# Rounding and clipping y through an int8 tile on ScalarE, with a new plan, in a cross-attention and BitNet-FFN kernel

## The chip, the cores and the metric

The kernel runs on one core of one Trainium2 chip. The core has five engines that matter here, each with its own instruction queue, executed in order: TensorE (PE; matmuls into PSUM), VectorE (DVE), ScalarE (ACT), GpSimd (POOL), and SyncE (SP), which here only issues DMA transfers. The metric is device time in microseconds (us). A "batch" below is one of 32 slices of 128x512 that pass through the whole network one after the other.

## What is computed

The input x has 32 batches of 128 channels x 512 positions; ctx has the same shape. Per batch:

```python
x = x + xattn(layernorm(x), ctx)      # 8 heads of 16 channels, 512 x 512 scores a head
x = x + ffn(layernorm(x))             # 128 rows, 512 -> 2048 -> 512

def act_quant(x):                     # 8 bits, one scale a row
    scale = 128 / clip(max|x|, 1e-5)
    return clip(round(x * scale), -128, 127) / scale

def ffn(x):
    gate, up = act_quant(x) @ wq(w_gate).T, act_quant(x) @ wq(w_up).T
    y = fwht(silu(gate) * up)         # Walsh-Hadamard transform over 2048
    return act_quant(y) @ wq(w_down).T
```

wq makes the weights ternary (-1, 0, 1) with one scale. The change concerns act_quant(y), the second rounding and clipping, and the multiplication by w_down.

## The kernel before

**Staging.** The work on each batch is cut into tasks, written as Python generators (`s_load`, `s_a`, `s_mpe`, `s_eact`, ... `s_dn`). Before each instruction or small block, a generator yields what it needs: a buffer of a ring (`"get"`), an event (`"on"`), or an engine and the duration that the planner should charge (`"pe", 0.234`; `"dma", 0.73`). The class `Plan` runs all generators together and keeps for each engine the time at which it would come free. At each step it takes the instruction that could start earliest; among those that could start within `eps` (`epspe` on PE) it takes the one of lowest rank. The rank is a number of the task from the table `CFG` (separate ones for the first four batches, `.h`, and the last four, `.z`) plus `T` times the batch; on PE the mode in which the array was last used is preferred by `stick`. This order is fixed when the program is built and becomes the order of every engine's queue. So `CFG` and the charged durations set the order of everything, and on the chip an engine can't overtake its own queue.

**Modes of PE.** Scores use two 48-row or 50-row strips of the array at once ("half"), the projections and the product with the values use quarter-column strips ("cols"), all else the whole array ("full").

**One batch on PE, by the names of the profile.** Projections of q and k (L556, L557) and v (L636) into `pf`. Scores are computed twice: `pS` (L726; 128 queries by 512 keys for two heads, of which DVE takes the maximum at L741; in the first three batches every other one goes through `pf` and L746 instead) and, transposed and with the maximum subtracted, `pT` (L796), which ACT turns into P by exp (L809). 16 of each a batch. `pav` (L830) is the product of P and v, eight blocks a batch. Then the output projection (L948), gate and up (L1013, WGQ and WUQ, four blocks each), the transposes of z (L1117), the Hadamard products (L1156, L1157), small transposes for the row maximum and its reciprocal (L1195, L1215, "yb"), and the down product (L1274, two blocks of eight). pS and pT have one buffer each, `pf` three, which nearly everything else shares.

**Around the change.** `s_yv` copies the transformed y (128 x 2048 floats, one buffer, ring `y`) from PSUM (L1171). `s_am` takes its row maximum on DVE (L1184). `s_q` multiplies y by the scale (L1232, POOL or DVE, in place, two halves of 1024). `s_q1` (L1242, ACT) adds 12582912, which rounds a float to an integer. `s_q2` (L1256, ACT) forms max(0, (12582912 + 127) - y), that is 127 minus the rounded and clipped value, and writes it as bf16 into `yq` (two buffers); only then is `y` free. `s_dn` multiplies yq by the ternary weights `WDQ`, and since every element is 127 minus what is wanted, one more matmul a batch (L1275) subtracts 127 times the column sums of the weights: `NEG` (2 rows of constants) times `CS` (the sums, split into two bf16 numbers). The result has the wrong sign, which a factor of -1 in the row scale (L1223) undoes. The column sums come once, after the weights are made ternary, from 16 matmuls (L502), four operations of DVE and one transfer (L506 to L515).

**The weights.** 12 tiles of 1 MB are loaded (`s_w`), their absolute values summed (L451), scaled and rounded (L475 on ACT or L477), clipped (L485) and converted to fp8 (L493). The first gate matmul waits for the last of them. Tiles use the rings z0, z1 and y, which the FFN needs later.

Of the kernel before, what the change touches and what calls it, by code (L numbers as in the profile page):

```python
# [10 lines left out]
F32 = mybir.dt.float32  # L11
FR = mybir.dt.float32r
BF = mybir.dt.bfloat16
F8 = mybir.dt.float8e4
AF = mybir.ActivationFunctionType
# [10 lines left out]
    "a": 17204.8,  # L26
    "a.h": 56888.9,
    "a.z": 14936.6,
    "a2": 4110.6,
    "a2.h": 10733.7,  # L30
    "a2.z": 4091.9,
    "a3": -1064.4,
    "a3.h": 4876.9,
    "a3.z": 2422.1,
    "am": 4773.1,
    "am.h": 13803.0,
    "am.z": -44218.1,
    "bf": 3144.9,
    "bf.h": 24712.8,
    "bf.z": 19590.3,  # L40
    "const": 14934.4,
    "const.h": 15491.8,
    "const.z": 4076.0,
    "dn": 4293.7,
    "dn.h": 4871.1,
    "dn.z": 21179.4,
    "eact": -36632.4,
    "eact.h": -37814.4,
    "eact.z": -1863.9,
    "eav": 11135.5,  # L50
    "eav.h": 4223.8,
    "eav.z": 32251.8,
    "epe": -40145.6,
    "epe.h": -40187.6,
    "epe.z": -39869.7,
    "gact": 23899.5,
    "gact.h": -26090.9,
    "gact.z": -36563.3,
    "gpe": 56880.8,
    "gpe.h": 18311.9,  # L60
    "gpe.z": 6005.8,
    "hi": -25784.5,
    "hi.h": -26246.1,
    "hi.z": 4960.2,
    "hm": -21491.6,
    "hm.h": -24541.6,
    "hm.z": -28755.2,
    "init": -37791.2,
    "init.h": -23577.8,
    "init.z": -24582.5,  # L70
    "lo": 1897.6,
    "lo.h": 4758.2,
    "lo.z": -37078.3,
    "load": 23789.4,
    "load.h": 4770.3,
    "load.z": -31350.6,
    "mdve": 1736.2,
    "mdve.h": 4251.6,
    "mdve.z": -25448.7,
    "mfin": -25604.8,  # L80
    "mfin.h": 4075.5,
    "mfin.z": 6355.4,
    "mpe": -26070.7,
    "mpe.h": -37503.9,
    "mpe.z": -21599.3,
    "o": -25785.8,
    "o.h": 35362.7,
    "o.z": -786.3,
    "o2": -37005.1,
    "o2.h": -41684.7,  # L90
    "o2.z": -24211.2,
    "q": 13848.2,
    "q.h": -39189.8,
    "q.z": 4318.1,
    "q1": 11956.7,
    "q1.h": 4753.0,
    "q1.z": 21160.0,
    "q2": 1023.0,
    "q2.h": -21667.4,
    "q2.z": -23754.1,  # L100
    "st": -47909.0,
    "st.h": -35889.1,
    "st.z": 21989.2,
    "u": 26418.5,
    "u.h": 5310.5,
    "u.z": 24337.0,
    "udve": 18718.4,
    "udve.h": 12493.6,
    "udve.z": -34405.8,
    "upe": 29615.8,  # L110
    "upe.h": 19928.1,
    "upe.z": 14589.9,
    "v": 27752.8,
    "v.h": 57650.1,
    "v.z": 53459.6,
    "w": 35469.7,
    "w.h": -19469.2,
    "w.z": 18308.4,
    "w1": 24353.6,
    "w1.h": 18083.3,  # L120
    "w1.z": -34718.8,
    "w2": 28388.6,
    "w2.h": 5547.9,
    "w2.z": 12473.5,
    "w3": 31248.0,
    "w3.h": 19526.9,
    "w3.z": 3962.9,
    "w4": 25647.7,
    "w4.h": 6555.5,
    "w4.z": 20517.4,  # L130
    "yv": -26156.9,
    "yv.h": 11959.1,
    "yv.z": 33180.6,
    "zt": 13824.7,
    "zt.h": 15480.3,
    "zt.z": -26679.3,
    "T": 5.6,
    "eps": 0.019,
    "pen": 9.6,
    "stick": 4685.6,  # L140
    "epspe": 0.21,
# [161 lines left out]
def xattn_ffn(  # L303
# [41 lines left out]
    MAG7 = const.tile([128, 1], F32, name="MAG7")  # L345
    nc.vector.memset(MAG7, MAGIC + 127.0)
# [10 lines left out]
    CW = const.tile([128, 388], F32, name="CW")  # L357
    WQ, WK, WVT, BRP, MASK = CW[:, 0:128], CW[:, 128:256], CW[:, 256:384], CW[:, 384:386], CW[:, 386:387]
    NEGC = CW[:, 387:388]
# [15 lines left out]

    ob = const.tile([128, 1], BF, name="ob")
    nc.vector.memset(ob, 1.0)
    NEG = const.tile([2, 128], BF, name="NEG")
    CS = const.tile([2, 512], BF, name="CS")
# [30 lines left out]
    def s_init():  # L410
        yield "on", "cw"
        yield "dve", 0.2
        nc.vector.tensor_scalar(NEG, ones[0:2, :], NEGC[0:2], None, ALU.mult)
# [17 lines left out]
    def s_w():  # L431
        for n in range(12):
            m, k = divmod(n, 4)
            src = srcs[m][0][k]
            yield "get", WR[n % 4]
            yield "dma", 2.9
            w = fp.tile([128, 2048], F32, name=WR[n % 4], bufs=2 if WR[n % 4] == "z0" else 1)
            nc.sync.dma_start(out=w.rearrange("p (j i) -> p j i", j=4) if m == 2 else w, in_=src)
            WT[n] = w
            p.marks["w", n] = p.done  # L440
            p.now = p.done - 2.9
# [46 lines left out]
    def s_w4():  # L488
        for n in range(12):
            m, k = divmod(n, 4)  # L490
            yield "on", "w3", n
            yield "act", 1.95
            nc.scalar.activation(srcs[m][1][:, k, :], WT.pop(n), AF.Identity, bias=NMAG, saturate=False)  # L493
            p.put(WR[n % 4])
            if k == 3:
                p.mark("wr", m)
        yield "get", "y"
        yield "get", "pf"
        yield "pe", 3.5
# [3 lines left out]
        yield "dve", 0.6  # L503
        w = fp.tile([128, 2048], F32, name="y")
        ca, cb = w[0:1, 0:512], w[0:1, 512:1024].bitcast(BF).rearrange("p (a f) -> p a f", a=2)
        nc.vector.tensor_scalar(ca, pc[0:1, :], 1.0 / 64.0, MAGIC, ALU.mult, ALU.add)  # L506
        yield "dve", 0.6, "port"
        nc.vector.tensor_scalar(cb[:, 0], ca, -MAGIC, None, ALU.add)
        yield "dve", 0.6, "port"
        nc.vector.tensor_scalar(ca, ca, -MAGIC, -64.0, ALU.add, ALU.mult)  # L510
        yield "dve", 0.6
        nc.vector.tensor_tensor(cb[:, 1], pc[0:1, :], ca, ALU.add)
        p.put("pf")
        yield "dma", 0.1
        nc.sync.dma_start(out=CS, in_=cb)  # L515
        p.now = p.done
        p.put("y")
        p.mark("cs")
# [19 lines left out]
    def s_load():  # L538
        for b in range(NB):
            s = st[b]  # L540
            yield "at", b
            yield "get", "xt"
            yield "get", "ct"
            yield "get", "cv"
            yield "dma", 0.73
            s["x"] = xp.tile([128, T], F32, name="xt")
            nc.sync.dma_start(out=s["x"], in_=x[b])
            yield "dma", 0.73
# [25 lines left out]
    def s_a2():  # L574
        for b in range(NB):
# [43 lines left out]
            yield "dma", 1.6, 0.45  # L619
            nc.sync.dma_start(out=xo[:, 1:4:2], in_=xf[:, 1:4:2])  # L620
            yield "dma", 1.6, 0.45
# [26 lines left out]
    def s_a3():  # L648
        for b in range(NB):
# [21 lines left out]
            yield "dma", 1.6, 0.45  # L671
            nc.sync.dma_start(out=xo[:, 0:4:2], in_=xf[:, 0:4:2])
            yield "dma", 1.6, 0.45
# [169 lines left out]
    def s_u():  # L843
        for u in range(NU):
# [26 lines left out]
            yield "dma", 0.73, 0.45, 0.7  # L871
# [14 lines left out]
    def s_o():  # L886
        for b in range(NB):
# [3 lines left out]
            if b in SHORT:  # L891
                yield "dma", 0.73, 0.45, 1.2
# [18 lines left out]
            yield "dma", 0.1, 0.45, 0.6  # L911
# [4 lines left out]
            yield "dma", 0.73, 0.45, 1.2  # L916
# [3 lines left out]
            yield "dma", 0.73, 0.45, 1.2  # L920
# [7 lines left out]
            yield "dma", 0.1, 0.45, -1.0  # L928
# [4 lines left out]
            yield "dma", 0.73, 0.45, 0.5  # L933
# [241 lines left out]
    def s_am():  # L1175
        for b in range(NB):
# [46 lines left out]
            nc.vector.tensor_scalar(yc, yc, SW[:, 2:3], -1.0, ALU.mult, ALU.mult)  # L1223
# [11 lines left out]
    def s_q1():  # L1235
        for b in range(NB):
            yield "at", b
            for hf in range(2):
                yield "on", "q", b, hf
                yield "act", 1.05  # L1240
                y = st[b]["y"][:, 8 * hf : 8 * hf + 8]
                nc.scalar.activation(y, y, AF.Identity, bias=MAG)  # L1242
                p.mark("q1", b, hf)

    def s_q2():
        for b in range(NB):
# [3 lines left out]
            for hf in range(2):  # L1250
# [5 lines left out]
                nc.scalar.activation(s["yq"][:, w], s["y"][:, w], AF.Relu, bias=MAG7, scale=-1.0)  # L1256
                p.mark("yq", b, hf)
            p.put("y")

    def s_dn():  # L1260
        for b in range(NB):
# [3 lines left out]
            if b == 0:  # L1265
                yield "on", "cs"
# [8 lines left out]
            nc.tensor.matmul(ps, NEG, CS, start=False, stop=True)  # L1275
# [7 lines left out]
            yield "dma", 0.73  # L1283
# [20 lines left out]
def _layout(i):  # L1304
# [12 lines left out]
    mask = np.zeros((128, 2), f)  # L1317
    mask[[48, 49, 112, 113], 0] = -1.0
    mask[0:2, 1] = -127.0 * 64.0, -127.0
# [34 lines left out]
```

## Time and profile before

| | |
|---|---|
| median of 3 runs | 1439.01 us (1437.6 to 1448.16) |
| the profiled execution | 1444.41 us, of it 1442.5 us between its first and last instruction (the span) |
| mean granted clock of TensorE | 0.95 |
| busy share of PE, DVE, ACT, POOL | 94%, 82%, 82%, 69% |
| transfers | 214 MB, 148 GB/s |
| L1275, the correction | 32 matmuls, 384 ns each |
| L502, the column sums | 16 matmuls, from 188.1 us on |
| L1242 and L1256, rounding and clipping | 64 each, 1138 ns each |
| last pS and last pT | 1313 us and 1359 us |

How to read it: times are from the first instruction on. Each row of a group gives the line, the engine, the operation, the tile written and the tiles read, and the shapes; then the total busy time, the mean of one, and how long the engine was idle just before. Matmuls are pipelined: the next starts before the former has ended, so the distance from start to start tells what one costs, not its duration. PEclk is the clock that the throttle granted to PE, in tenths. The chain of waits follows the execution back from its last instruction, at each step to what released it.

### The profile page before, as it was taken

What the parts mean: (1) busy time and instruction counts of PE and PEld (TensorE: products, weight loads), DVE (VectorE), ACT (ScalarE), POOL (GpSimd) and SP (SyncE); (2) the same over time, 40 slices, a digit from 0 to 9 for tenths busy, and PEclk for the clock granted to TensorE, in tenths of its full rate; (3) what the DMA queues carried; (4) which work ended last, traced back from release to release, by engine and by line L of the source; (5) the groups of instructions that cost most, each with busy time, mean ns of one, the idle gap of its engine ahead of it and who ended that gap; (6) DMA issues with size and microseconds to landing.
All of it is one profiled execution on the core that took longest, in us unless ns stands there. A gap on an engine that the chain in (4) does not pass through costs nothing.

```text
span 1442.5 us, 21845 instructions
## 1 busy us (share of the span) xinstructions
PE 1353.4 (94%) x7454; PEld 529.8 (37%) x7454; DVE 1179.0 (82%) x1759; ACT 1189.0 (82%) x1574; POOL 994.7 (69%) x781
## 2 busy tenths in 40 slices
PE   3788899999999999999999999999999999999875
PEld 2222233433334333333333344333333343433332
DVE  2875878888898889888888888888888888886784
ACT  5688978888888888888888888888888888889643
POOL 3122229977777777887777787887777788769550
PEclk7596899999999999999999999999999999999986
DMA  8967555555445555555545555555554554321000
GB/s 285 282 201 245 158 159 160 151 152 143 134 147 163 171 171 174 161 153 148 136 134 154 171 167 175 168 162 156 137 141 140 161 166 153 95 65 49 21 15 15
DMA packets 136315, 214.15 MB, mean 148 GB/s; under 512 B 36746, under 2 KB 38924, under 8 KB 135180
## 3 DMA queue, kind: packets, MB, share of 16 engines
q1 hardware_dynamic: 136204, 212.75, 49.7%
q8 instruction: 59, 0.97, 0.3%
q14 instruction: 52, 0.43, 0.1%
HBM read 106.94 MB, written 93.31 MB: 139 GB/s over the span
## 4 chain that ended last, share of the span: by engine, by line
PE 84%; DVE 7%; ACT 4%; DMA 2%; issue 2%; POOL 0%; SPq 0%; ACTq 0%; DVEq 0%; POOLq 0%
PE pav L830 17%; PE pf L1013 15%; PE pT L796 14%; PE pS L726 10%; PE pf L1274 8%; PE pf L1117 4%; PE pf L556 4%; PE pf L1156 3%; ACT P L809 2%; DVE M L741 2%; PE pf L1157 2%; PE pf L948 2%; PE pf L636 2%; DVE ya L1184 1%; PE pf L1275 1%
## 5 line engine op out<-in xcount | busy, mean ns | idle before, releaser
L741 DVE TENSOR_REDUCE M<-pS 128x2 f32<-128x1024 f32 x488 | 595.0, 1219 | 105.0 <-PE pS L726 103.1
L1097 POOL TENSOR_TENSOR z<-z 128x512 f32<-128x512 f32 x491 | 619.0, 1283 | 68.5 <-DVE z L1068 48.5
L809 ACT ACTIVATE P<-pT 128x1024 f32<-128x1024 f32 x512 | 523.2, 1022 | 148.2 <-PE pT L796 146.4
L830 PE MATMUL pav<-P,va 128*32 128x512 f32 x2048 | 283.6, 625 | 0.0
L796 PE MATMUL pT<-qs,ks 50*128 50x512 f32 x1024 | 259.0, 500 | 17.1 <-ACT P L809 16.5
L726 PE MATMUL pS<-ks,qs 48*128 48x512 f32 x976 | 227.2, 458 | 14.8 <-DVE M L741 9.9
L796 PEld LDWEIGHTS pT<-qs,ks 50*128 50x128 f32 x1024 | 98.1, 188 | 240.3 <-ACT P L809 149.9
L1232 POOL TENSOR_TENSOR y<-y,YB 128x1024 f32<-128x1024 f32 x60 | 140.9, 2369 | 34.9 <-ACT YB L1218 34.9
L1013 PEld LDWEIGHTS <-xqT 128*128 128x128 bf16 x1024 | 91.8, 100 | 155.7 <-issue 84.8
L726 PEld LDWEIGHTS pS<-ks,qs 48*128 48x128 f32 x976 | 95.3, 190 | 117.8 <-issue 39.6
L532 POOL TENSOR_TENSOR arstd<-arstd,MHALF 128x1 f32<-128x1 f32 x32 | 18.6, 580 | 170.4 <-DVE arstd L529 134.8
L1013 PE MATMUL pf<-WGQ,xqT 128*128 128x512 fp8e4 x512 | 133.4, 386 | 1.0 <-ACT z L1043 0.6
L1274 PE MATMUL pf<-WDQ,yq 128*128 128x512 fp8e4 x512 | 125.4, 389 | 8.6 <-ACT yq L1256 8.5
L1184 DVE TENSOR_REDUCE ya<-y 128x128 f32<-128x1024 f32 x64 | 127.1, 1986 | 6.6 <-ACT y L1171 6.3
L1013 PE MATMUL pf<-WUQ,xqT 128*128 128x512 fp8e4 x512 | 127.0, 381 | 0.1
L1068 DVE TENSOR_TENSOR z<-z,pf 128x512 f32<-128x512 f32 x128 | 84.6, 675 | 12.9 <-PE pf L1013 8.7
L1140 DVE TENSOR_TENSOR lo<-pf,hi 128x512 fp32r<-128x512 f32 x128 | 85.7, 675 | 6.0 <-ACT hi L1129 5.9
L1043 ACT ACTIVATE z<-pf,tk 128x512 f32<-128x512 f32 x128 | 83.7, 685 | 7.4 <-PE pf L1013 4.7
L1129 ACT CAST hi<-pf 128x512 fp32r<-128x512 f32 x128 | 74.6, 588 | 17.9 <-PE pf L1117 17.9
L1171 ACT COPY y<-pf 128x512 f32<-128x512 f32 x128 | 71.9, 585 | 13.6 <-PE pf L1157 13.3
L1117 PE MATMUL pf<-CM,z 128*128 128x128 f32 x512 | 82.0, 286 | 0.0
L1274 PEld LDWEIGHTS <-yq 128*128 128x128 bf16 x512 | 46.1, 99 | 89.7 <-ACT yq L1256 22.5
(129 smaller groups left out, 1791.5 us busy)
## 6 DMA issues: line engine op xcount, KB each, us to landing
xd<-X SPq DMA_DIRECT2D x128, 512.0 KB
qs<-xd SPq DMA_DIRECT2D x128, 192.0 KB
ks<-xd SPq DMA_DIRECT2D x128, 192.0 KB
ud<-U SPq DMA_DIRECT2D x62, 256.0 KB
xt<-x SPq DMA_DIRECT2D x32, 256.0 KB
ct<-cx SPq DMA_DIRECT2D x32, 256.0 KB
RR<-R SPq DMA_DIRECT2D x64, 128.0 KB
xr<-x SPq DMA_DIRECT2D x32, 256.0 KB
```

Of the source, the lines that this page charges most:

```text
L726: nc.tensor.matmul(ps[e], qs[w, t, bass.ts(qt, 128)], ks[w, t, :], start=True, stop=True)
L741: nc.vector.tensor_reduce(m, ps[2], AX.X, ALU.max)
L796: nc.tensor.matmul(ps[:, e], ks[w, t, bass.ts(kt, 128)], qs[w, t, :], start=True, stop=True)
L809: nc.scalar.activation(P, TQ[u, n], AF.Exp, scale=0.25)
L830: nc.tensor.matmul(av[32 * h : 32 * h + 32, :], va[:, kt, 4 * hf + h, :], P[:, e], start=(kt == 0), stop=(kt == 3),)
L1013: nc.tensor.matmul(ps, xqT[:, k, :], W[:, k, bass.ts(c, 512)], start=(k == 0), stop=(k == 3))
L1097: E[p.eng].tensor_tensor(ix(dv, k), ix(av, 0), ix(av, 1), o)
L1117: nc.tensor.transpose(ps[:, i, :], st[b]["z"][:, bass.ts(4 * c + i, 128)], EYE)
L1140: nc.vector.tensor_tensor(t, F.pop(("z", b, c)), F["hi", b, c].bitcast(F32), ALU.subtract)
L1184: nc.vector.tensor_reduce(ya[:, h], s["y"][:, 8 * h : 8 * h + 8].rearrange("p j t -> p t j"), AX.X, ALU.max, apply_absolute_value=True,)
L1232: E[p.eng].tensor_tensor(y, y, st[b]["YB"].to_broadcast([128, 8, 128]), ALU.mult)
L1274: nc.tensor.matmul(ps, s["yq"][:, j, :], WDQ[:, j, :], start=(j == 0), stop=False)
```

## The change

The first of the two passes of ACT now copies the scaled y into an int8 tile `yi` (new, one buffer), and the conversion does the rounding and the clipping. The second copies `yi` to bf16. yq then holds the values themselves, so `NEG`, `CS`, the column sums, the correction matmul and the factor -1 go. `y` is free after the first pass instead of the second. The durations that the planner charges for most transfers are raised (a 256 KB tile 0.73 to 0.85, a weight tile 2.9 to 3.5, the stores of xd 1.6 and 0.45 to 1.7 and 0.9), some landing times are changed, and all numbers of `CFG` are new, `T` and `eps` among them.

```diff
 CFG = {
-    "a": 17204.8,
...
-    "T": 5.6,
-    "eps": 0.019,
-    "pen": 9.6,
-    "stick": 4685.6,
-    "epspe": 0.21,
+    "a": 21145.3,
...
+    "T": 65.3,
+    "eps": 0.0,
+    "pen": 36.3,
+    "stick": 12961.1,
+    "epspe": 0.23,
 }
...
-            yield "dma", 2.9
+            yield "dma", 3.5
             w = fp.tile([128, 2048], F32, name=WR[n % 4], bufs=2 if WR[n % 4] == "z0" else 1)
...
-        yield "get", "y"
-        yield "get", "pf"
-        yield "pe", 3.5
-        pc = ps_f.tile([128, 512], F32, name="pf")
-        for j in range(NI):
-            nc.tensor.matmul(pc[0:1, :], ob, WDQ[:, j, :], start=(j == 0), stop=(j == NI - 1))
...
-        nc.sync.dma_start(out=CS, in_=cb)
-        p.now = p.done
-        p.put("y")
-        p.mark("cs")
...
-            yield "dma", 0.73
+            yield "dma", 0.85
             s["x"] = xp.tile([128, T], F32, name="xt")
...
-            yield "dma", 1.6, 0.45
+            yield "dma", 1.7, 0.9
             nc.sync.dma_start(out=xo[:, 1:4:2], in_=xf[:, 1:4:2])
...
-            nc.vector.tensor_scalar(yc, yc, SW[:, 2:3], -1.0, ALU.mult, ALU.mult)
+            nc.vector.tensor_scalar(yc, yc, SW[:, 2:3], None, ALU.mult)
...
                 yield "on", "q", b, hf
+                if hf == 0:
+                    yield "get", "yi"
                 yield "act", 1.05
-                y = st[b]["y"][:, 8 * hf : 8 * hf + 8]
-                nc.scalar.activation(y, y, AF.Identity, bias=MAG)
+                if hf == 0:
+                    st[b]["yi"] = fp.tile([128, NI, 128], I8, name="yi", bufs=RINGS["yi"])
+                w = slice(8 * hf, 8 * hf + 8)
+                nc.scalar.copy(st[b]["yi"][:, w], st[b]["y"][:, w])
                 p.mark("q1", b, hf)
+            p.put("y")
...
-                nc.scalar.activation(s["yq"][:, w], s["y"][:, w], AF.Relu, bias=MAG7, scale=-1.0)
+                nc.scalar.copy(s["yq"][:, w], s["yi"][:, w])
                 p.mark("yq", b, hf)
-            p.put("y")
+            p.put("yi")
...
-                yield "pe", 1.73 + 0.22 * g
+                yield "pe", 1.73
                 for j in range(8 * g, 8 * g + 8):
-                    nc.tensor.matmul(ps, s["yq"][:, j, :], WDQ[:, j, :], start=(j == 0), stop=False)
-            nc.tensor.matmul(ps, NEG, CS, start=False, stop=True)
+                    nc.tensor.matmul(ps, s["yq"][:, j, :], WDQ[:, j, :], start=(j == 0), stop=(j == NI - 1))
```

More of the change, by code (lines that the diff above doesn't have):

```diff
@@ L14 @@
 F8 = mybir.dt.float8e4
+I8 = mybir.dt.int8
 AF = mybir.ActivationFunctionType
@@ new lines @@
+    "a.h": -13181.5,
+    "a.z": 1173.4,
+    "a2": -17104.5,
+    "a2.h": 690.4,
+    "a2.z": 42446.1,
+    "a3": -3175.8,
+    "a3.h": -8664.4,
+    "a3.z": 16459.6,
+    "am": 161.0,
+    "am.h": 17364.9,
+    "am.z": 32182.3,
+    "bf": 18683.0,
+    "bf.h": 31269.3,
+    "bf.z": 35303.2,
+    "const": -5501.7,
+    "const.h": 37755.7,
+    "const.z": 1763.1,
+    "dn": 239.1,
+    "dn.h": -21980.0,
+    "dn.z": 42699.2,
+    "eact": -7602.6,
+    "eact.h": -40084.8,
+    "eact.z": -1227.4,
@@ new lines @@
+    "eav": -18087.6,
+    "eav.h": -36108.9,
+    "eav.z": 38280.9,
+    "epe": -45496.9,
+    "epe.h": -38542.2,
+    "epe.z": -33211.5,
+    "gact": -4441.9,
+    "gact.h": 32995.2,
+    "gact.z": -46212.5,
+    "gpe": 53791.6,
+    "gpe.h": 14740.7,
+    "gpe.z": 54572.1,
+    "hi": -15301.6,
+    "hi.h": -5849.9,
+    "hi.z": 53342.2,
+    "hm": 18328.4,
+    "hm.h": -17814.5,
+    "hm.z": -41074.9,
+    "init": -43982.4,
+    "init.h": -42277.6,
+    "init.z": -13781.6,
+    "lo": -34328.7,
@@ new lines @@
+    "lo.h": -4433.6,
+    "lo.z": -40564.4,
+    "load": -36992.5,
+    "load.h": -44212.0,
+    "load.z": 43264.4,
+    "mdve": 999.3,
+    "mdve.h": -35953.7,
+    "mdve.z": 18143.4,
+    "mfin": -13986.7,
+    "mfin.h": -6279.4,
+    "mfin.z": -13213.6,
+    "mpe": -38114.1,
+    "mpe.h": -37525.8,
+    "mpe.z": -42237.2,
+    "o": -6480.8,
+    "o.h": 16244.1,
+    "o.z": 34116.5,
+    "o2": -36848.5,
+    "o2.h": -12371.4,
+    "o2.z": -12361.7,
+    "q": 36512.0,
+    "q.h": -15314.2,
+    "q.z": -41040.2,
@@ new lines @@
+    "q1": 42319.9,
+    "q1.h": 18458.6,
+    "q1.z": -5657.8,
+    "q2": -8876.8,
+    "q2.h": 21172.4,
+    "q2.z": 16920.5,
+    "st": -39351.8,
+    "st.h": -11680.5,
+    "st.z": -37439.4,
+    "u": -6996.8,
+    "u.h": -5670.2,
+    "u.z": -7564.8,
+    "udve": -3685.7,
+    "udve.h": 16214.8,
+    "udve.z": -38407.0,
+    "upe": 8177.0,
+    "upe.h": 31488.8,
+    "upe.z": 36033.6,
+    "v": 30497.8,
+    "v.h": -4196.4,
+    "v.z": -47392.4,
+    "w": 37879.4,
+    "w.h": -40543.6,
+    "w.z": -13715.2,
@@ L142 @@
+    "w1": 18646.4,
+    "w1.h": 31573.4,
+    "w1.z": -36044.3,
+    "w2": 42721.7,
+    "w2.h": 36222.1,
+    "w2.z": -43436.0,
+    "w3": 53243.0,
+    "w3.h": 42675.6,
+    "w3.z": -42266.9,
+    "w4": -77.4,
+    "w4.h": -36686.9,
+    "w4.z": -36683.9,
+    "yv": -6876.1,
+    "yv.h": -3275.6,
+    "yv.z": 52586.2,
+    "zt": 1199.1,
+    "zt.h": -3401.9,
+    "zt.z": -47936.5,
+    "T": 65.3,
[3 more added lines that the diff above has]
+    "epspe": 0.23,
 }
@@ L344, in xattn_ffn @@
     nc.vector.memset(NMAG, -MAGIC)
-    MAG7 = const.tile([128, 1], F32, name="MAG7")
-    nc.vector.memset(MAG7, MAGIC + 127.0)
     zeros = const.tile([128, 1], F32, name="zeros")
@@ L355, in xattn_ffn @@
     kss = [sp.tile([128, 2, T], FR, name=f"ks{i}") for i in range(4)]
-    CW = const.tile([128, 388], F32, name="CW")
+    CW = const.tile([128, 387], F32, name="CW")
     WQ, WK, WVT, BRP, MASK = CW[:, 0:128], CW[:, 128:256], CW[:, 256:384], CW[:, 384:386], CW[:, 386:387]
-    NEGC = CW[:, 387:388]
     CM = const.tile([128, 642], F32, name="CM")
@@ L374, in xattn_ffn @@
     SW = const.tile([128, 3], F32, name="SW")
[L376 to L379, printed above, removed]
     p = Plan(nc, RINGS, CFG)
@@ L440, in s_w @@
             p.marks["w", n] = p.done
-            p.now = p.done - 2.9
+            p.now = p.done - 3.5
     def s_w1():
```

153 lines of the change are left out of this document (14 added, 139 removed), and 2 rows, old and new, of the table RINGS.

## The prediction

> **What bounds the kernel now.** I read the page's busy shares and slices first, then the stages, then TensorE's rows in one steady batch, then the chain of waits.
>
> ```profile
> PE 1353.4 (94%) x7454; PEld 529.8 (37%) x7454; DVE 1179.0 (82%) x1759; ACT 1189.0 (82%) x1574; POOL 994.7 (69%) x781
> ...
> PE   3788899999999999999999999999999999999875
> ...
> PEclk7596899999999999999999999999999999999986
> ```
>
> TensorE (PE) is full from the sixth slice to the last but three. The stage table (columns: stage, its length, then busy time and count by engine, clock, DMA share, GB/s) says how full:
>
> ```profile
> 0.00:250.00 250.00, 196.75 (x948) 70.28 (x949) 170.12 (x261) 194.66 (x235) 88.41 (x81) 0.80 0.68 214
> 250.00:1300.00 1050.00, 1047.85 (x6014) 413.29 (x6012) 913.60 (x1349) 907.57 (x1222) 834.88 (x649) 1.00 0.52 150
> ...
> 1358.60:1442.50 83.90, 55.63 (x221) 25.88 (x219) 55.45 (x86) 41.28 (x58) 24.40 (x16) 0.79 0.03 13
> ```
>
> So a head of 250 us at a clock of 0.80, 1,050 us in which PE idles 2 us, and a tail of 84 us after the last transposed score (at 1358.65). A busy PE isn't PE at its peak, so I price it by start-to-start distances. From the timeline of the steady part:
>
> ```profile
> 713.16 0.40 PE L726 MATMUL pS<-ks,qs 48*128 48x512 f32 x2
> 713.49 1.06 PE L830 MATMUL pav<-P,va 128*32 128x512 f32 x8
> ...
> 717.64 0.39 PE L1275 MATMUL pf<-CS,NEG 2*128 2x512 bf16 x1
> 717.96 0.50 PE L796 MATMUL pT<-qs,ks 50*128 50x512 f32 x2
> ```
>
> A score block (two matmuls, pT or pS) advances PE by 0.33 us in a run of such blocks, a pav block by 1.00, the correction matmul by 0.32 (717.64 to 717.96). The correction stands at 717.64 in one batch and at 757.80 in the next: 40.1 us a batch. Pricing every block so, with its mode switch, gives 39.7 us a batch, so only 0.4 us is waiting; over the whole kernel it gives 1279 us, the rest being about 91 us of waiting and half clock in the head, 14 in the middle, 45 from 1300 on, and 8 before the first matmul. **The bound is PE's own order**; what comes free on ScalarE (ACT) doesn't shorten it.
>
> **The change, part by part.** All sums are against the profiled execution: 1442.5 us span, 1444.4 with what lies around it, 5.4 above the median of the runs (1439.0).
>
> *Removed on PE.* 32 corrections x 0.32 = 10.2 us, all on the saturated engine. The 16 column-sum matmuls (L502) start at 188.11 and the next score at 191.66: 3.5 us, and the score it holds back is waited for by the exp. Sum **-13.7**. The four VectorE (DVE) operations and the 2 KB transfer behind the column sums, and two memsets, lie beside this; nothing.
>
> *The two ACT passes.* They stay 64 + 64 of 128x1024. L1242 and L1256 took 1138 ns each, with a bias tile. No row has a float-to-int8 or int8-to-bf16 pass. Bounds: 1053 (L451, absolute value of 1024 floats) and 2 x 585 = 1170 (two 512-wide copies from PSUM, L1171); at most 2369, what GpSimd needs for 1024 (L1232). I take 1.06. ACT then frees 128 x 0.08 = 10 us, off the path: ACT idled in the steady part for want of PE's scores (80.9 us between 400 and 1130). At 2369 it would add 158 us to ACT, 4.9 a batch on top of some 35 of 40, and ACT would become the bound; the conversion is one pass of the same engine over as many elements, so I leave that to a rival. [...]
>
> *y comes free a pass earlier.* L1232, L1242 and L1256 work on a single y. After the change the first pass releases it, 1.1 us (one pass) sooner. In the steady part PE isn't waiting for y, so nothing; in the last three or four batches about 1.1 us each, **-4**.
>
> *The order.* The priorities of every task and the planner's transfer prices change too, so every queue is reshuffled. I laid the two programs' PE lists side by side and priced each block as above.
>
> - Work per batch is the same blocks less one. But there are 223 lone score blocks instead of 158; a lone one advances PE by 0.43 (a pT at 728.93, the next block at 729.36), 0.10 more than in a run: +6.8. Quarter-column blocks straight after full-array ones go from 24 to 52 at 0.09: +2.6. Other switches +0.3. Sum **+9.7**.
> - Scores closer than their consumers allow. pT and pS have one buffer each. The chain shows the shortest turn of each:
>
> ```profile
> 87.63 0.45 PE pT L796 x2
> 88.08 0.02 issue
> 88.10 1.03 ACT P L809
> 89.13 0.04 issue
> 89.18 0.50 PE pT L796 x2
> ...
> 173.05 0.45 PE pS L726 x2
> 173.49 0.02 issue
> 173.51 1.24 DVE M L741
> 174.75 0.04 issue
> 174.80 0.51 PE pS L726 x2
> ```
>
> pT to pT 1.55 us, pS to pS 1.75. I summed PE's own work between successive ones, from the first gate matmul on. Before: 3 pT gaps and no pS gap under 1.45, 37 pS gaps of 1.45 to 1.75; shortfalls 1.6 us (pT) and 2.6 (pS). After: 21 and 12, many of 0.66 (score pairs in a row with nothing between them, around pT 127 to 135 and 401 to 407 of 512), and 146 pS gaps of 1.45 to 1.75; shortfalls 9.7 and 19.8. Behind a waiting score stands all of PE. The increase is 17 us by pS alone, 25 if the pT shortfalls never coincide with them: **+20**. The old order in the middle lost 14 where the gaps alone said 4, so it may be more; if PE's order was drawn where it idles anyway, less: 8 to 30.
>
> *Head.* Same weights, same 54 exps before the first silu; the w_down loads go to SP's queue ahead of the fifth batch's inputs and that batch's RR swap, and 4.9 us more attention precedes the first gate matmul. About 30 of the head's 91 us aren't explained by score turns, and PE's waits that name a DMA are 12 (CW 7.8, ks 4.4). CW comes first in both. Bounds -12 and +8, taken as **0**, since the ks waits are small and more weight loads ahead delay inputs.
>
> [...]
>
> *Tail.* The last pT has 10.8 us less PE work before it, but 4 instead of 3 batches still have their y scaling to come (28 instead of 29 yb transposes done, 49.8 instead of 44.5 us of PE work left). One batch at the end takes 20 us. That is a wash: 84 us becomes 84 to 95 with the last pT earlier by 10.8. With y free earlier: PE's idle here goes from 39 to about 35, the -4 above.
>
> Sum: -13.7 + 9.7 + 20 + 0 - 4 = **+12**, and 4 more for the 4.4 us by which the head's score turns grow by the same count (63.9 instead of 59.5): **+16**. Span 1458, median of the runs 1439 + 16 = **1455**.
>
> **Rivals.**
>
> 1. *The corrections' saving is kept* (ends not slower). It decides if the head reordering is worth 12 or more, because inputs are asked for when the traces say they land, and the shortfalls cost 8: -13.7 + 9.7 + 8 - 12 - 4 + 4 = -8, 1431; with the shortfall at 14, 1437. For it: 0.68 DMA share and a 0.80 clock in the head. Against: only 12 us of PE's waits there name a DMA.
> 2. *Rings add to the bunched scores.* Three pf buffers serve every block but the scores and pav; where attention runs ahead, ACT's exps delay the FFN copies that free them. Shortfalls at 30 and a tail of 95 us (+7): -13.7 + 9.7 + 30 + 4 + 7 = +37 at worst; 1470 at half of that excess. For it: the measured 14 against 4.
> 3. *The int8 passes aren't priced like others.* At 1.2 us more a pass ACT is full; 32 x 2 to 4 us gives 1500 and more. Nothing in the trace points there.
>
> **How the numbers follow.** Forecast 1455 (1442 to 1466): chance 0.55, about 0.33 of it beyond +1%. Rival 1: 0.28, of which 0.08 is below -1% and the rest within. Rival 2: 0.15. Rival 3: 0.02. One per cent is about what a measurement of this kernel can tell from no change (1424.6 to 1453.4). So faster 0.08, same 0.42, slower 0.50. The range takes in most of rivals 1 and 2: 1431 to 1472. The likeliest case sits close to the line between same and slower.
>
> **What would show it.** No L1275 and L502, their 13.7 us gone. Both passes near 1.06 us. PE idle, or long pT and pS advances, in the middle where attention bunches, with ACT named for pT and DVE for pS; a steady batch of 40.3 to 41.2 us instead of 40.1. Last pT at 1365 to 1380. The forecast is wrong if the middle runs at 39.7 a batch or less, if the first gate matmul comes well before 186, or if the tail after the last pT is under 75 us.

## The result, and the profile after

The changed kernel takes **1519.5 us** (median of 4 runs, 1515.2 to 1526.6); the kernel before took 1441.3 beside it (1437.6 to 1448.2). The ratio is 1.054, with a 95% interval of 1.048 to 1.060: 78 us slower. The forecast of 1455 had the right side and missed the size; 1519 lies far outside its range of 1431 to 1472. The profiled execution of the changed kernel took 1519.85 us, 1518.0 of it the span, 75.5 more than the span before.

In the page after, the busy shares and the slices that answer to those shown of before:

```profile
PE 1373.5 (90%) x7406; PEld 535.4 (35%) x7406; DVE 1185.5 (78%) x1753; ACT 1197.1 (79%) x1575; POOL 992.2 (65%) x779
...
PE   3788799999899999999999999999899999998475
...
PEclk7578899999999999999999999999999999999786
```

No engine has more to do in any way that matters: DVE, ACT and POOL are busy for the same time within 1%, and PE's 20 us more come with 48 matmuls fewer, so its matmuls last longer in the record (185.5 ns in the mean instead of 181.6). All shares fall because the span grew. So the 75.5 us are waiting, apart from what more switches of PE's mode may cost. The last three digits of the PE row (475) say where some of it is: a hole in the tail.

The stage table of after, cut at the first gate matmul and at the start of the last pT (columns: stage, its length, busy time and count of PE, PEld, DVE, ACT, POOL, then clock, DMA share, GB/s):

```profile
0.00:196.60 196.60, 135.60 (x641) 47.65 (x642) 125.27 (x192) 152.62 (x179) 47.87 (x46) 0.74 0.71 232
196.60:1395.80 1199.20, 1166.76 (x6504) 453.76 (x6502) 989.95 (x1461) 995.59 (x1325) 900.49 (x704) 1.00 0.46 139
1395.80:1518.00 122.20, 71.18 (x262) 34.02 (x262) 70.31 (x101) 48.89 (x71) 43.88 (x30) 0.76 0.03 11
```

The same cuts in the kernel before are at 185.7 and 1358.7 of 1442.5; its first two rows (the third stands in the prediction):

```profile
0.00:185.70 185.70, 133.60 (x604) 46.44 (x604) 121.75 (x188) 145.39 (x172) 47.91 (x46) 0.73 0.74 236
185.70:1358.60 1172.90, 1164.17 (x6633) 457.44 (x6631) 1001.80 (x1485) 1002.28 (x1345) 922.36 (x719) 1.00 0.50 144
```

So the loss splits in three:

| stage | before | after | difference |
|---|---|---|---|
| head, to the first gate matmul | 185.7 | 196.6 | +10.9 |
| middle, to the last pT | 1172.9 | 1199.2 | +26.3 |
| tail, after it | 83.9 | 122.2 | +38.3 |

In the steady stretch one batch after the other has the same length. The row of the small transpose yb (L1184), of which there is one a batch, in a window of the steady stretch, after and (L1215) before:

```profile
L1184 PE MATMUL pf<-CM,yb x5: 328/332/332, 822.8 to 989.4; 128*128 128x128 f32 x5
...
L1215 PE MATMUL pf<-CM,yb x5: 329/330/330, 820.1 to 980.7; 128*128 128x128 f32 x5
```

From the first to the fifth are four batches in 166.6 us, **41.65 a batch**; the forecast said 40.3 to 41.2, and it was 40.15 before.

The new passes are where they were expected (rows of L1215 and L1230: minimum, median and maximum in ns, first and last start):

```profile
L1215 ACT CAST yi<-y x64: 1028/1045/1071, 261.1 to 1506.1; 128x1024 int8<-128x1024 f32 x64
...
L1230 ACT CAST yq<-yi x64: 1027/1044/1068, 264.8 to 1508.0; 128x1024 bf16<-128x1024 int8 x64
```

The forecast's own value was 1.06. Which of the two sides is int8 makes no difference that these rows show.

**The tail.** What PE and the others wait for in it (waits after 1395.8: who, for whom, us in total, times, longest):

```profile
PE pf L1248 <- ACT yq L1230: 28.4, 6, 16.8
DVE lo L1109 <- ACT hi L1098: 20.8, 3, 16.6
ACT yi L1215 <- POOL y L1201: 19.9, 5, 17.4
```

Three long waits of about 17 us, on three engines, that end one in the other: the second half of a down product waits for yq, whose pass stands behind yi on ACT, and yi waits for POOL's scaling of y. In the tail of the kernel before, the longest wait for yq (of PE's weight loads; 17.0 here) is 5.3 us:

```profile
PEld L1274 <- ACT yq L1256: 8.7, 2, 5.3
```

The timeline of after (start, us, engine, line, operation) shows why:

```profile
1394.43 2.37 POOL L1201 TENSOR_TENSOR y<-y,YB 128x1024 f32<-128x1024 f32 x1
1396.76 17.74 POOL L1066 TENSOR_TENSOR z<-z 128x512 f32<-128x512 f32 x14
1414.45 2.34 POOL L1201 TENSOR_TENSOR y<-y,YB 128x1024 f32<-128x1024 f32 x1
...
1398.34 1.04 ACT L1230 CAST yq<-yi 128x1024 bf16<-128x1024 int8 x1
1416.83 1.04 ACT L1215 CAST yi<-y 128x1024 int8<-128x1024 f32 x1 [17.44 <-POOL y L1201]
```

Between the two halves of one batch's scaling stand 14 butterflies of a later batch in POOL's queue. POOL works through them first, 17.74 us in all, ACT waits 17.4 us with its next copies queued behind, and y, of which there is one buffer, stays taken. The distance from one yb transpose to the next, 27.1, 21.1 and 20.4 us at the end of the kernel before, is here 48.1, 25.4, 22.8 and 18.9, with four batches to go instead of three.

**The head.** The last tile of w_down is scaled at 176.5 and clipped at 179.4 before. After (timeline, two queues):

```profile
184.88 2.10 ACT L466 ACTIVATE y<-y,MAG,SC 128x2048 f32<-128x2048 f32 x1
...
187.71 0.75 DVE L849 SCALAR_TENSOR_TENSOR x<-pf,BO,xr 128x512 f32<-128x512 f32 x1 [0.56 <-PE pf L917]
...
191.77 1.78 DVE L476 TENSOR_SCALAR y<-y 128x2048 f32<-128x2048 f32 x1
```

The scaling starts 8 us later, in an ACT queue that is busy with exps and copies ahead of it, and the clip stands for 5 us in DVE's queue behind the residual sum (L849), its statistics and two maxima. That is this tile's place in the two queues; DVE idles less than 1 us between.

The first gate matmul doesn't wait for this tile itself on the chip, though. It reads only w_gate's weights and xqT, and the rows of PE just ahead of it are these:

```profile
195.71 0.81 PE L695 MATMUL pS<-ks,qs 48*128 48x512 f32 x2 [0.50 <-DVE M L710]
196.46 0.38 PE L732 MATMUL pf<-CM,M 128*16 128x128 f32 x1
196.63 0.63 PE L982 MATMUL pf<-WGQ,xqT 128*128 128x512 fp8e4 x1
```

It starts when the blocks ahead of it in PE's queue are through. The tile counts by way of the order: the generator of the gate waits for the event that the last w_down tile is converted, and by the planner's clock that event moved from 171.2 to 186.8, so more attention was put ahead of the gate. From the last sum over w_down's absolute values (148.8 before, 153.2 after, 151.0 and 155.4 in two other profiles of the same head) to the first gate matmul PE has 134 matmuls in 36.9 us before and 173 in 43.3 after: 4.7 us more of advance and 1.7 more of idle time. In the unshortened profiles of the new order without the correction this stretch takes 43.3 to 43.8. The other 4.4 us lie ahead of it; the largest difference there is PE's wait for the absolute sums of w_gate near 30 us, 11.7 us (L448) against 3.4, which is only 6.9 in another profile of the same head.

### The profile page after: what moved, and what is told of

It reads as the page before. It is cut to its first block, busy times and chain, and to the rows that moved or that the text cites. A ratio compares the mean times of both kernels' runs of the same rounds, so it can differ in the third digit from the quotient of the medians.

```text
span 1518.0 us, 21675 instructions
## 1 busy us (share of the span) xinstructions
PE 1373.5 (90%) x7406; PEld 535.4 (35%) x7406; DVE 1185.5 (78%) x1753; ACT 1197.1 (79%) x1575; POOL 992.2 (65%) x779
## 5 line engine op out<-in xcount | busy, mean ns | idle before, releaser
L1066 POOL TENSOR_TENSOR z<-z 128x512 f32<-128x512 f32 x489 | 616.9, 1284 | 66.4 <-DVE z L1037 41.2
L695 PE MATMUL pS<-ks,qs 48*128 48x512 f32 x976 | 235.8, 476 | 24.7 <-DVE M L710 16.5
L1153 DVE TENSOR_REDUCE ya<-y 128x128 f32<-128x1024 f32 x64 | 126.8, 1981 | 11.0 <-ACT y L1140 10.9
L908 POOL TENSOR_TENSOR N<-N,RB 128x512 f32<-128x512 f32 x31 | 39.6, 1278 | 97.7 <-DMA RB<-rd 62.6
L501 POOL TENSOR_TENSOR arstd<-arstd,MHALF 128x1 f32<-128x1 f32 x32 | 19.4, 606 | 128.1 <-DVE arstd L498 124.7
L1086 PE MATMUL pf<-CM,z 128*128 128x128 f32 x512 | 86.1, 290 | 13.2 <-DVE xq L947 5.2
L1037 DVE TENSOR_TENSOR z<-z,pf 128x512 f32<-128x512 f32 x128 | 86.1, 677 | 14.3 <-PE pf L982 13.7
L1012 ACT ACTIVATE z<-pf,tk 128x512 f32<-128x512 f32 x128 | 84.3, 683 | 10.4 <-PE pf L982 9.6
L1140 ACT COPY y<-pf 128x512 f32<-128x512 f32 x128 | 75.5, 591 | 19.6 <-PE pf L1126 18.8
```

What stands on the lines that cost most here:

```text
L695: nc.tensor.matmul(ps[e], qs[w, t, bass.ts(qt, 128)], ks[w, t, :], start=True, stop=True)
L1037: nc.vector.tensor_tensor(zc, zc, F.pop(("u", b, c)), ALU.mult)
L1066: E[p.eng].tensor_tensor(ix(dv, k), ix(av, 0), ix(av, 1), o)
L1153: nc.vector.tensor_reduce(ya[:, h], s["y"][:, 8 * h : 8 * h + 8].rearrange("p j t -> p t j"), AX.X, ALU.max, apply_absolute_value=True,)
```

## The experiments

Two kinds are used. In the first, the order of every queue is kept and only the instructions in it change: the generators yield exactly what they yielded, so the planner decides the same. In the second, the planner's input is changed and the order is drawn anew.

**The arithmetic in the old order.** The kernel before, with all its yields; the passes, the factor and the down product are those of the changed kernel, and the instructions of the column sums are dropped (their durations stay in the plan).

```diff
-                y = st[b]["y"][:, 8 * hf : 8 * hf + 8]
-                nc.scalar.activation(y, y, AF.Identity, bias=MAG)
+                nc.scalar.copy(st[b]["yi"][:, w], st[b]["y"][:, w])
...
-                nc.scalar.activation(s["yq"][:, w], s["y"][:, w], AF.Relu, bias=MAG7, scale=-1.0)
+                nc.scalar.copy(s["yq"][:, w], s["yi"][:, w])
...
-            nc.tensor.matmul(ps, NEG, CS, start=False, stop=True)
```

> The order of every queue stays that of the kernel before; only the arithmetic changes: int8 tile, copy to bf16, no correction matmul, no column sums, factor +1. Theory A (the loss lies in the new order, the arithmetic itself gains): 1441 less 10.2 (32 corrections at 0.32) less 3.5 (column sums) = 1427.5, and up to 4 less where y comes free a pass earlier in the tail, so 1423 to 1430; tail after the last pT 80 to 84 us, first gate matmul near 185. Theory B (the int8 passes or the earlier release of y cost the time): 1480 or more. Theory C (PE waits elsewhere, so that taking 13.7 us of matmuls out brings nothing): 1438 to 1444.

Measured: **1429.8 us** against 1442.4 of the kernel before beside it, ratio 0.992 (0.989 to 0.995). The stage table of its profile:

```profile
0.00:183.70 183.70, 130.81 (x605) 44.94 (x606) 121.56 (x187) 145.11 (x172) 47.79 (x46) 0.75 0.74 238
183.70:1350.00 1166.30, 1154.17 (x6589) 453.77 (x6587) 998.97 (x1481) 995.42 (x1345) 921.49 (x719) 1.00 0.51 145
1350.00:1432.80 82.80, 53.95 (x216) 25.67 (x215) 55.33 (x86) 39.62 (x58) 24.39 (x16) 0.79 0.04 13
```

All three stages are a little shorter than before, none is longer. So the new arithmetic by itself is a gain of some 12 us, the new order a loss of 90 (1519.5 - 1429.8), and theory A holds. It is also the version that beats both kernels.

**The correction alone.** The same, but with the old two passes; the output, with no correction, is too large by 127 column sums.

```diff
-            nc.tensor.matmul(pc[0:1, :], ob, WDQ[:, j, :], start=(j == 0), stop=(j == NI - 1))
...
-            nc.tensor.matmul(ps, NEG, CS, start=False, stop=True)
```

> The order of the kernel before with its own two passes of ScalarE; only the correction matmul and the column sums (with their four VectorE operations and the transfer) are left out, so the output is 127 times the column sums too large. Theory A: 1427 to 1431, that is 10 to 14 below the kernel before, and 0 to 4 above the run with int8 in the old order. If the int8 passes gain or lose by themselves, the two runs differ by more than 5. Theory C: 1438 to 1444.

Measured: 1431.7 us, ratio 0.993 (0.991 to 0.996). So 10.7 of the 12.6 us come from the matmuls, and the int8 path adds 1.9, which the two intervals don't tell from nothing. The commonest distance between two yb transposes goes from 40.1 to 39.8, one correction of 0.32 (in the mean of nine batches, from 40.2 to 40.0).

**The correction put back into the new order.** The column sums follow at once on the last w_down tile.

```diff
+                nc.scalar.activation(s["yq"][:, w], s["yi"][:, w], AF.Relu, bias=P127, scale=-1.0)
...
+            nc.tensor.matmul(ps, NEG, CS, start=False, stop=True)
```

> The order of the changed kernel; the correction matmul, the column sums and the factor -1 are put back, the second pass forms 127 minus the int8 value with a bias tile. Theory A (the correction costs the same in either order): 1519.5 + 10 to 14 = 1529 to 1534. Rival (in the new order PE waits so much that a correction fits into the waits): 1519 to 1524.

Measured: 1539.8 us, 20 more than the changed kernel and 6 more than the top of what theory A expected. The steady batch grows by 0.3 (41.7 to 42.0), which is the correction; the first gate matmul comes at 205.0 instead of 196.6, which is more than the 3.5 us of the column sums. In this place they also take one of the three pf buffers that the plan had not set aside; how much that does was not tried. The rival falls: the correction doesn't fit into the waits.

**The y scaling in the tail.** From the 28th batch on, both halves go to DVE and are planned as one step.

```diff
             for hf in range(2):
-                yield ("pool", "dve"), (2.33, 1.14), "port"
+                if hf == 0 or b < NB - 5: yield ("pool", "dve") if b < NB - 5 else "dve", (2.33, 1.14) if b < NB - 5 else 2.28, "port"
```

> The changed kernel; from the 28th batch on both halves of the scaling of y go to VectorE, charged as one step, so that they don't stand in GpSimd's queue with 14 butterflies between them. All queues are the same up to there. Theory T1 (the 38 us by which the tail grew are mostly that one place: yi waits 17.4, the down product 16.8): the tail after the last pT goes from 122 to 104 to 110, the time to 1502 to 1508. Theory T2 (the tail is long because four batches instead of three still had their y to do, whatever the order of the scaling): 1515 to 1522.

Measured: **1496.9 us**, 22.7 less than the changed kernel. Its tail in the stage table, and its longest wait of the down product there:

```profile
1391.20:1491.90 100.70, 65.97 (x262) 30.90 (x262) 72.71 (x104) 47.63 (x71) 38.56 (x29) 0.83 0.04 13
```

```profile
PEld L1248 <- ACT yq L1230: 10.0, 4, 5.1
```

The tail is 21.5 us shorter (122.2 to 100.7), the 17-us waits are gone, and the yb distance of 48.1 is 28.7. So 19.4 of the 21.5 us came back at that one distance. T1 holds, with more than it promised. The edit also changes the engine: a half takes 1.22 us on DVE and 2.36 on POOL, which may be in the other 2 us and in a little of the 19.4. Against 83.9 before, 17 us of the tail remain.

**Short turns of pS.** The maximum runs over half the keys, and a filler keeps DVE busy (1209.5 us in all instead of 1185.5).

```diff
-                    nc.vector.tensor_reduce(m, ps[2], AX.X, ALU.max)
+                    nc.vector.tensor_reduce(m, ps[2][:, :, 0:256], AX.X, ALU.max)
+                    nc.vector.tensor_reduce(FIL, ROPE[:, :, 0:256], AX.X, ALU.max)
```

> The changed kernel, order unchanged; the maximum of each pS is taken over 256 of the 512 keys, so half of it is left out, and a second VectorE instruction of the same size reads a constant tile instead, so that VectorE stays as busy and only pS comes free some 0.6 us sooner (turn 1.75 to about 1.2). Theory S (the middle lost its time to pS blocks that stand closer together than one turn): the steady batch goes from 41.7 to 40.2 or less, 14 such batches and the two bunches give 20 to 30 us, 1490 to 1500. Rival (the steady batch is longer for another reason, the work or the turn of pT): the batch stays above 41.2, the time above 1508.

> The same edit in the kernel before, as the control. Theory S: its pS blocks are far enough apart, the batch stays at 39.8 to 40.1 and the time at 1436 to 1442. If a shorter turn brings as much here as in the new order, theory S falls.

Measured: 1509.2 us in the new order, 10.4 less; 1442.0 in the old one, against 1441.8 unchanged (ratio 0.999 to 1.003). The batch in the new order, from the yb row of a steady window (here L1186), is 164.1 / 4 = 41.03:

```profile
L1186 PE MATMUL pf<-CM,yb x5: 330/332/332, 819.8 to 983.9; 128*128 128x128 f32 x5
```

The batch lies between the two expectations, the time on the rival's side of 1508: the control bears the theory out, but the amount is half of the least that it promised. When each advance of PE is set against its price, the steady batch of the changed kernel waits 1.93 us (0.45 ahead of pS, 0.30 ahead of pav, 0.11 ahead of pT, 0.48 ahead of the transposes of z); with the short pS turn it waits 1.30, and pT now has 0.63 of it. So a part of the second wait stood behind the first.

**Both turns short.** DVE as before with a filler of the right size; on ACT the exp covers one of the two heads of a pT.

```diff
-                nc.scalar.activation(P, TQ[u, n], AF.Exp, scale=0.25)
+                nc.scalar.activation(P[:, 0], TQ[u, n][:, 0], AF.Exp, scale=0.25)
+                nc.scalar.activation(AB[:, 0:240], ROPE[:, 0, 0:240], AF.Exp, scale=0.25)
...
-                            P[:, e],
+                            P[:, 0],
```

> The changed kernel, order unchanged. The maximum of pS is taken over 256 of 512 keys, and the exp over one of the two heads of each pT (the other head's half is left out and the product with the values reads the first head's P twice); a filler on each engine, on constant tiles, brings its time back to what it was (1.22 and 1.03). So only the two turns are shorter (about 1.2 and 1.1 us). Short pS turns alone took 10.4 us (1509 against 1519.5) and left 41.0 a batch, with the late blocks now pT (0.63 a batch). Theory S2 (that rest is the turn of pT, hidden behind pS before): the batch goes to 40.2 to 40.5, the time to 1496 to 1503. Rival (the rest of the excess comes from the transposes of z that wait for GpSimd, and from pf): 40.8 or more, 1505 or more.

> The same edit in the kernel before, as the control. Theory S2: 39.8 to 40.1 a batch, 1432 to 1442, since its scores stand far enough apart in the steady part and only the head and the bunch near the end can gain.

Measured: 1480.8 us in the new order, 38.7 less than the changed kernel; 1428.4 in the old order, 14.0 less than the 1442.4 beside it and below the range expected of it. The steady batch of the new order (three batches, 120.4 us) is 40.13:

```profile
L1187 PE MATMUL pf<-CM,yb x4: 328/331/332, 840.0 to 960.4; 128*128 128x128 f32 x4
```

The middle goes from 1199.2 to 1163.8 in the new order and from 1172.9 to 1166.9 in the old (rows of the two runs):

```profile
190.60:1354.40 1163.80, 1137.40 (x6505) 439.12 (x6504) 945.37 (x1901) 932.84 (x1785) 899.57 (x704) 1.00 0.50 144
...
177.80:1344.70 1166.90, 1152.97 (x6633) 446.62 (x6631) 954.07 (x1927) 953.82 (x1808) 923.12 (x719) 0.99 0.51 145
```

So the turns of the scores cost the new order 35.4 us in the middle and the old one 6.0: **29 us** is what the new order lost there, more than S2 asked for, and with the turns away its middle is even 3 us shorter than the old one's, with 10.2 us of corrections less and, by the forecast's count, some 10 of mode switches more. The fillers left DVE with 4.5% and ACT with 6.3% less to do in the middle of the new order (ACT 932.8 instead of 995.6), so a part of the effect may be that; the control, both engines 4.8% lighter, gains 6 in its middle. Short turns of pT alone were not tried.

**The last butterflies short.** As above, and the last two butterflies of each half do half of their elements.

```diff
-                ix = lambda v, k: v[:, k] if n == 1 else v[:, :, k]
+                h = slice(0, 64) if i == 3 else slice(None)
+                ix = lambda v, k: v[:, k] if n == 1 else v[:, :, k, h]
```

> As the run with both turns short in the new order, and the last two of the butterflies of each half work on half of their elements (the others are left out), so that the last one before the transposes of z ends 1.2 us sooner. If the transposes that wait for GpSimd (13.1 us in ten steady batches of the changed kernel as weight loads, 0.48 a batch as lost time) are a part of the loss: the batch is 0.3 to 0.5 shorter than with the two turns alone, some 8 us in the time. If it is only the next thing behind the scores: no change.

Measured: 1469.6 us in one run. The steady batch is the same as with the turns alone, 40.12 us in both, with 0.31 still waited ahead of the transposes of z. So the length of POOL's last butterflies, which the wait rows name there, doesn't by itself decide when they start; the 9.8 us between the two spans are 2.1 in the head, 4.3 in the middle outside the steady stretch, and 3.4 in the tail. What the transposes wait for is open.

**The planner's inputs.** The old code with the new durations of transfers, the new code with the old ones, and the new code with one of them old.

```diff
-            yield "dma", 3.5
+            yield "dma", 2.9
```

> The kernel before with its own table and arithmetic; only the durations that the planner charges for transfers are the new ones. Theory O (an order is only good with the table that was drawn for these durations; any other input scatters it): no steady batch at all, 1550 to 1640. Theory N (the new durations, which are closer to the traces, make a better order by themselves, and the new table loses): 1420 to 1445.

> The changed kernel with its new table; only the durations charged for transfers are the old ones. Theory O: scattered like the other, slower than the changed kernel, 1540 to 1590. Theory N: 1519 or less, if the new durations carry the loss. For the head: if the later first gate matmul (196 instead of 186) comes from the charge of 3.5 for a weight tile, it returns to 183 to 188 here.

> The changed kernel with one number changed: a weight tile is charged 2.9 instead of 3.5 as before. The tests on the charge: with all transfer charges old, the first gate matmul came at 180.9 instead of 196.6. If the charge of the weight tiles decides that, it comes at 178 to 185 here; if the other charges do, at 192 or later. Theory O also says that the rest of the order is scattered by this one number: no steady batch, 1550 to 1580.

Measured, one run each: 1623.2, 1566.1 and 1567.7 us. In none is there a steady stretch: yb distances in the middle of the third are 38.5, 44.1, 41.6, 39.6, 39.0, 47.2, 41.9, 66.3. Theory O holds. Neither set of durations is shown to be the better one by itself; the table of ranks fits one set of them, and even one number scatters the order. The head does follow the charge: first gate matmul at 180.9 and 183.2 where a weight tile costs 2.9, at 194.5 to 199.4 in four profiles of the new order with 3.5. But the old table with 3.5 has it at 187.2, so it is the charge together with the new table. By the planner's clock the last w_down tile is converted at 169.7, 170.1, 186.8 and 182.9 in these, which is the event that the gate's place follows.

**What is left of the tail.** One rank changed (36512 to 0, ahead of the butterflies):

```diff
-    "q": 36512.0,
+    "q": 0.0,
```

> The changed kernel with one number of its table changed: the rank of the y scaling goes from 36512 to 0, ahead of the butterflies; the queues are the same up to about the 24th batch. Theory M (the rest of the longer tail is one more batch left after the last pT): three batches are left instead of four, the tail is 80 to 86, the last pT comes 5 to 10 us later than 1392 to 1396, the time 1490 to 1500. Rival (the rest of the tail is waiting inside each of the last batches): the tail stays at 95 or more.

Measured: 1502.2 us, 17 less than the changed kernel. Three batches are left after the last pT, as in the kernel before; the tail is 91.5, not 80 to 86, and the last pT comes at 1409.4, 18 us later than in the run with the scaling on DVE. Neither theory holds: against that run the batch fewer is 9 us of the tail, and it was paid for twice over ahead of it. Against the changed kernel the tail is 30.6 us shorter and the last pT 13.5 later.

**Both causes away.** Short turns of both scores and the y scaling on DVE.

> The two edits together: short turns of pS and pT as in e9 (the same parts left out), y scaling first from the 28th batch on as in e4. If the causes are separate they add up: 1480.8 - 22.7 = 1458, tail 100. The old order with short turns took 1428.4; the 30 left are then the head (10 to 13) and the batch more in the tail (17 to 20). If they hid each other: 1465 or more, or under 1450.

Measured: 1455.7 us (1458 expected), tail 99.0, middle 1166.0. The two causes add up, so they are separate. Against the old order with short turns (1428.4) 27 us are left, by stage in the two profiles: head 187.2 against 177.8, middle 1166.0 against 1166.9, tail 99.0 against 83.6. The head and the rest of the tail are all that is left.

## Why the prediction was wrong, point by point

- **Removed on PE, -13.7.** Held, a little high: 10.7 us for the matmuls, 12.6 with the rest, in the old order.
- **The ACT passes, 1.06 us and off the path.** Held: 1045 and 1044 ns.
- **y free a pass earlier, -4.** Not seen as such. The old order with the int8 path is 1.9 us faster than with only the matmuls out. In the new order y was held 17 us longer by a queue, which no early release makes good.
- **Mode switches, +9.7.** Not read by itself. With both turns short the new order's steady batch is 40.13, and the old one's without the corrections 39.8 (40.0 in the mean): 0.1 to 0.3 more, at most 10 us over 32 batches. But 0.31 of that batch is still the wait ahead of the transposes of z, which can be all of it.
- **Bunched scores, +20 (8 to 30).** Right in kind, at the upper end in size: 29 us by the two runs with both turns short. It put most of it on pS, and with pS's turn alone taken away only 10.4 us came back in the whole time: the two waits stand behind one another.
- **Head, 0 (-12 to +8).** Wrong: +10.9. This step saw 4.9 us more attention ahead of the first gate matmul and still took the whole as nothing, against up to 12 us of waits for transfers that might go. The stretch of PE's queue in question is 6.4 us longer (4.7 of it advance), and nothing was gained ahead of it to set against that: the part before is 4.4 longer too. It didn't ask why the gate had moved back: the last w_down tile, which the gate follows in the planner's order, has its scaling and its clip behind other work of ACT and DVE.
- **Tail, "a wash", 84 to 95.** The step that failed most: +38.3. It priced the tail by the PE work left in it. The end of this kernel isn't PE's: 21.5 us went when the last y scalings left POOL's queue, 19.4 of them at the one half that stood behind 14 butterflies, and the forecast didn't read that queue to the end. That there was one batch more to do was seen and set against an earlier last pT, which came 37 us later (1395.8 instead of 1358.65).
- **The clock around the column sums.** In the kernel before, the granted clock was 0.50 from 181.1 to 187.9 us, 7 us, and 1.00 from there. In the old order without the sums (the run with the int8 passes) it is 0.88 at 175 to 180, 0.50 at 180 to 184, 0.79 at 184 to 188 and 1.00 from there to 200, which adds up to some 7 us at half as well. So no longer stretch at half clock is seen where they are out.
- **Rival 1** (the corrections' saving is kept, 1431) gives the time of the old order with the new arithmetic, 1429.8; as a forecast of this change it was out, since the order changed too. **Rival 2** named a longer tail and more of the bunched scores, and was far too small. **Rival 3** is out by the ACT rows.
- **The sums.** The parts given for the 1442.5 us (1279, 91, 14, 45 and 8) add up to 1437, so 5.5 us stand in none, and half of rival 2's excess gives 1466, not 1470. Neither moves the forecast.

The sum, stage by stage of the profiles: head 10.9, middle 26.3, tail 38.3. Of the middle, 6.6 is saved by the arithmetic (1172.9 to 1166.3 in the old order) and 32.9 lost by the order, 29 of them by the turns of the scores. What stays open is the price of the new order's head, which no run took away, and 15 to 17 us of the tail: one more batch and the waiting inside the last four were not separated.

**What the kernel knew.** The time at which the last of the computing engines comes free by the planner's own clock, which the forecast didn't use, stands here beside the spans on the chip:

| order | planner's end | span | difference |
|---|---|---|---|
| kernel before | 1396.0 | 1442.5 | 46.5 |
| changed kernel | 1478.3 | 1518.0 | 39.7 |
| its y scaling on DVE at the end | 1462.6 | 1491.9 | 29.3 |
| its rank of the y scaling 0 | 1459.1 | 1500.9 | 41.8 |
| old code, new durations | 1571.8 | 1621.4 | 49.6 |
| new code, old durations | 1522.3 | 1564.3 | 42.0 |
| new code, weight tile at 2.9 | 1521.4 | 1565.9 | 44.5 |

The planner gives the changed kernel 82 us more, the chip 75.5. It also has the parts: first gate matmul 171.2 and 187.1, steady batch 39.7 and 41.3, tail 71.5 and 105.2. It can't tell the two variants of the tail apart (3.5 us the other way round), but for a difference of 80 it was enough, and it was to be had without the chip.

## What to carry to other kernels

When an edit comes with a new schedule, price the two separately: put the new instructions into the old order and see what they do (here -12 us), and treat the order as a change of its own (here +90). Read every engine's queue to its end, those of lightly loaded engines too, and ask of each instruction that stands between the two halves of a job what the second half holds up. Where a planner made the order, read its own clock first, stage by stage.

## What the runs showed that was not expected

One waiting place hides the next: taking pS's turn away gave 10.4 us and moved 0.5 us a batch to pT; taking both gave 38.7. One cause alone measured a quarter of what the two were worth together (pT's alone was not tried).

DVE and POOL both took longer in one place where they worked at the same time on tiles in SBUF. The row of the y scaling in the run with the scaling on DVE (minimum, median, maximum):

```profile
L1201 DVE TENSOR_TENSOR y<-y,YB x10: 1216/1220/2304, 1390.0 to 1478.6; 128x1024 f32<-128x1024 f32 x10
```

A half takes 1.22 us. At 1390.02 one ran in 1.219. POOL started five butterflies at 1390.18 and was through with them 8.23 us later, which at 1.28 each, the median in the changed kernel, would be 6.4; the next half on DVE, started at 1391.16, took 2.304. What holds the two up there was not shown by any run.

A single number of the planner's input, 2.9 instead of 3.5 for a weight tile that is used twelve times at the start, moved the whole time by 48 us (1567.7 against 1519.5), more than the edit of the arithmetic did in any order.
